# A graph network's neighbour sums on TensorE: from two column halves of up to 64 nodes to four column quarters of up to 32

## The chip, the cores and the metric

The kernel runs on one core of a Trainium2 chip. The metric is the device time of one execution in microseconds. Before the change three runs took 2215.41, 2216.05 and 2217.56 us, median 2216.05 us.

## The reference

There are 6250 nodes with 512 features each and 106,250 directed edges (50,000 random ones in both directions and a loop at every node). Two layers follow each other. Each takes, for every node, the mean of its neighbours' rows, multiplies the mean and the node's own row with a 512 x 512 matrix each, and normalises.

```python
edge_index = jnp.stack([src, dst])
# layer 0
x_l = x @ W_l.T + b_l
agg = segment_sum(x_l[src], dst, num_segments=N_NODES)
deg = segment_sum(ones, dst)
x = _layernorm(x + agg / maximum(deg, 1)[:, None] + x @ W_r.T)
# layer 1: src and dst change roles
msg = h[dst] @ W_neigh.T + b_neigh
neigh = segment_sum(msg, src) / maximum(deg, 1)[:, None]
out = relu(h @ W_self.T + b_self + neigh)
x = _layernorm(h + layernorm(h + out) * ln_gamma + ln_beta)
```

All is in float32. A sum over edges of a product is the product of the sum, so the kernel sums the raw rows first and multiplies the means afterwards. Only the order of the sums differs from the reference.

## The kernel before

The edges are sorted by their target node, and cut into 831 tiles of 128 edges. `place` (L357) finds the first node of every run of seven tiles (`SPAN`), checks that a run meets at most 64 nodes (`H`), and writes a flag; if the flag is not zero, the slow path `plain` is taken, which the data here never does. There are 119 runs. A group `g` is run `g` together with run `60 + g`, so there are 60 groups a layer.

`grouped` (L460) works group by group. For a group:

- `fetch` (L482) gathers the neighbours' rows: one indirect DMA on GpSimd's queue (POOL) for each tile, 128 rows of 2 KB. Seven gathers fill one `rows` buffer; there are six (`CHUNKS`), that is three groups' worth. A gather into a buffer waits until TensorE has read what was there.
- `match` (L495), on VectorE, makes the 0/1 matrices `hot` that say which edge belongs to which of the run's 64 nodes. It reads `s.rel`, which `place` wrote, and the row numbers in PSUM tile `misc`.
- `own_rows` (L534) loads the nodes' own rows through SP's queue, two issues of 64 rows whose start is read from a register.
- `visits` (L547), on TensorE, multiplies `hot` with the rows: 8 tiles for each run (its seven, and the last one of the run before, since a node's edges may begin there). Run `g` uses the left half of TensorE's columns and run `60 + g` the right half, writing to partitions 0 to 63 and 64 to 127 of `agg`. Each float32 matmul is two passes in the trace.
- `shrink` (L502), on ScalarE, makes a bf16 copy of `hot`, and `count` (L560) multiplies it with ones: eight small matmuls give the degrees, in two columns of `misc`.
- `inverse` on VectorE and `average` (L570) on ScalarE make the mean, `turn` (L577) transposes own rows and means on TensorE (eight transposes, `tp`), and `dense` (L582) multiplies both with the weights: 16 passes into `po`.
- `store` (L586) runs `finish0` or `finish1` on VectorE (bias, residual, layer norms) and writes the rows out through SP, two issues of 64 rows. A window may write rows that belong to the next run and that a later group writes again. The last group of each column half writes by an indirect DMA on POOL instead.

The order is written out by hand; each engine executes its own instructions in that order. In turn `g` of the loop (L618) stand: fetch and match of group `g + 1`, own rows, visits, count and average of `g`, at most one step of the other layer's sort that uses TensorE, dense of `g - 1`, turn of `g`, store of `g - 1`, shrink of `g + 1`, up to five sorting steps on VectorE. The sort of layer 1's edges (`Sorter.runs`) is spread over layer 0's groups in this way. VectorE therefore runs, per turn: match of `g + 1`, inverse of `g`, finish of `g - 1`, sorting steps.

Layer 1 gathers from `h_d`, which layer 0 writes, so its first gather waits for layer 0's last store. All of POOL's gathers are issued in program order, and each uses one of eight semaphores in turn, so it also waits for the eighth gather before it to land.

## Time and profile before

| what | value |
|---|---|
| median of three runs | 2216.05 us |
| the profiled execution | 2719.07 us |
| its span, first to last instruction | 2717.3 us |
| TensorE matmul busy | 2071.7 us (76%) |
| TensorE weight loads busy | 861.5 us (32%) |
| VectorE busy | 1047.1 us (39%) |
| ScalarE busy | 390.2 us (14%) |
| GpSimd (POOL) busy | 1594.0 us (59%), 1679 instructions |
| first gather starts at | 28.2 us |
| last gather of layer 0, first of layer 1 start at | 1318.0, 1369.7 us |
| last gather of layer 1 starts at | 2641.0 us |
| mean granted clock of TensorE | 0.899 |

The profiled execution is 503 us longer than the median. Durations below come from it.

How to read the lines: in a group's line stand the source line, the engine, the operation, what it writes and reads, partitions and elements, and the number of instructions; behind the first bar the busy time in us and the mean ns of one; behind the second the idle time of the engine before them, and who ended most of it. PE is TensorE's matmul, PEld its weight load, DVE is VectorE, ACT ScalarE. `128*64` is a matmul on 128 rows and 64 columns of the array. In the order of time stand the start in us, the busy time, the engine, the line, and in brackets the idle time before it and its releaser. `issue` means that the engine waited for nothing that the trace shows. In a chain of waits stand who waited for whom, the us in total, how many times, and the longest.

### The profile page before, as it was taken

The page shows a single profiled execution, that of the slowest core. Times are in us where ns is not written, and L with a number is a line of the kernel's source. Part 1 is how long each engine was busy: PE and PEld are TensorE (multiplying, and loading weights), DVE is VectorE, ACT ScalarE, POOL GpSimd, SP SyncE. Part 2 cuts the span into 40 slices and gives each one's busy share as a digit, 9 for nine tenths or more (in the row PEclk, how much of TensorE's full clock was granted, in tenths as well). Part 3 has the DMA queues.
Part 4 walks back from the last instruction along what each step waited for, and adds up shares of the span by engine and source line. Part 5 has one row for each costly group of instructions (what it writes and reads, how often), then busy time and mean ns, then how long its engine had stood idle before and what let it go on. Part 6 is the DMA issues. An engine that isn't in the chain of part 4 may idle for free.

```text
span 2717.3 us, 23134 instructions
## 1 busy us (share of the span) xinstructions
PE 2071.7 (76%) x7807; PEld 861.5 (32%) x7807; DVE 1047.1 (39%) x2139; ACT 390.2 (14%) x685; POOL 1594.0 (59%) x1679
## 2 busy tenths in 40 slices
PE   2488887778787878888927777778777887877785
PEld 1133333333333333333303333333333333333332
DVE  1344434443434443222302444444444444444444
ACT  0111111111111111111101111111111111111111
POOL 4566665556666565666265566665666666656650
PEclk8789988888898989999968998999899899988998
DMA  7576766666666666676366666666666666666650
GB/s 225 164 204 192 204 199 187 184 182 190 190 191 192 184 196 185 196 214 207 106 178 175 189 192 199 202 201 197 187 202 199 203 200 187 195 189 196 202 174 19
DMA packets 177784, 508.07 MB, mean 187 GB/s; under 512 B 35564, under 2 KB 38054, under 8 KB 177646
## 3 DMA queue, kind: packets, MB, share of 16 engines
q0 software_dynamic: 133456, 437.13, 55.5%
q1 hardware_dynamic: 41358, 63.76, 7.3%
q10 hardware_dynamic: 2832, 5.51, 0.6%
q8 instruction: 66, 1.08, 0.2%
q14 instruction: 72, 0.59, 0.1%
HBM read 475.03 MB, written 31.46 MB: 186 GB/s over the span
## 4 chain that ended last, share of the span: by engine, by line
issue 23%; DVE 9%; PE 8%; SPq 7%; DMA 1%; ACT 1%; another core or an unknown queue 1%; POOLq 0%
PE po L456 6%; SPq L543 4%; SPq L598 2%; DVE po L170 2%; DVE stats L402 2%; SPq L509 2%; DVE po L408 1%; PE tp L447 1%; DVE po L424 1%; DVE po L427 1%; DMA own<-h_d 1%; DVE y L170 1%; PE agg L555 1%; ACT rstd L406 0%
## 5 line engine op out<-in xcount | busy, mean ns | idle before, releaser
L478 POOL DMA_INDIRECT rows<-in_x_dram,idx x831 | 797.0, 959 | 492.3 <-PE agg L555 240.3
L478 POOL DMA_INDIRECT rows<-h_d,idx x831 | 788.7, 949 | 482.5 <-PE agg L555 246.8
L555 PE MATMUL agg<-rows,hot 128*64 128x512 f32 x3792 | 918.2, 613 | 37.9 <-issue 21.7
L456 PE MATMUL po<-wb,ownT 128*128 128x512 f32 x960 | 574.2, 754 | 7.3 <-DVE y L170 6.3
L555 PEld LDWEIGHTS agg<-rows,hot 128*64 128x64 f32 x3792 | 293.8, 140 | 580.4 <-issue 536.8
L456 PE MATMUL po<-wa,meanT 128*128 128x512 f32 x960 | 431.5, 592 | 0.0
L565 PE MATMUL misc<-ones_b,hotb 128*128 128x1 bf16 x960 | 41.5, 164 | 349.1 <-issue 225.7
L456 PEld LDWEIGHTS po<-wb,ownT 128*128 128x128 f32 x960 | 222.2, 243 | 261.3 <-issue 260.1
L424 DVE SCALAR_TENSOR_TENSOR po<-bn,some,po 128x512 f32<-128x512 f32 (+1 forms) x60 | 45.3, 756 | 605.0 <-PE tp L447 264.0
L456 PEld LDWEIGHTS po<-wa,meanT 128*128 128x128 f32 x960 | 181.6, 189 | 234.0 <-issue 234.0
L449 ACT COPY ownT<-tp 128x512 f32<-128x512 f32 x120 | 69.9, 582 | 971.4 <-PE tp L447 497.6
L414 DVE SCALAR_TENSOR_TENSOR po<-bl_t,some,po 128x512 f32<-128x512 f32 (+1 forms) x60 | 45.2, 753 | 406.4 <-PE agg L555 212.9
L574 ACT ACTIVATE mean<-agg,inv 128x512 f32<-128x512 f32 x120 | 82.4, 687 | 788.9 <-DVE some L441 319.6
L438 DVE TENSOR_SCALAR inv<-misc 128x1 f32<-128x1 f32 x120 | 18.9, 158 | 425.7 <-remote 312.2
L170 DVE SCALAR_TENSOR_TENSOR srt<-srt 128x448 f32<-128x448 f32 (+2 forms) x310 | 180.2, 623 | 3.9
L565 PEld LDWEIGHTS <-hotb 128*128 128x128 bf16 x960 | 40.8, 99 | 443.9 <-issue 268.7
L447 PE MATMUL tp<-ident,mean 128*128 128x128 f32 x480 | 77.9, 288 | 123.0 <-ACT mean L574 112.1
L170 DVE SCALAR_TENSOR_TENSOR hot<-rel,misc 128x1024 f32<-128x1024 f32 x120 | 145.2, 1211 | 0.2 <-DVE misc L468 0.2
L447 PE MATMUL tp<-ident,own 128*128 128x128 f32 x480 | 76.0, 276 | 67.5 <-issue 39.3
L504 ACT CAST hotb<-hot 128x1024 bf16<-128x1024 f32 x120 | 123.5, 1029 | 22.6 <-DMA bn<-in_L_gnn_b_neigh_dram 16.1
L406 ACT ACTIVATE rstd<-mv,eps 128x1 f32<-128x1 f32 x180 | 53.0, 295 | 464.0 <-DVE mv L404 343.6
L447 PEld LDWEIGHTS tp<-ident,mean 128*128 128x128 f32 x480 | 58.9, 148 | 131.8 <-ACT mean L574 119.8
(111 smaller groups left out, 841.3 us busy)
## 6 DMA issues: line engine op xcount, KB each, us to landing
own<-h_d SPq DMA_DIRECT2D x119, 128.0 KB
own<-in_x_dram SPq DMA_DIRECT2D x117, 128.0 KB
h_d<-y SPq DMA_DIRECT2D x116, 128.0 KB
out_dram<-y SPq DMA_DIRECT2D x116, 128.0 KB
rows<-in_x_dram,idx POOLq DMA_INDIRECT x831
rows<-h_d,idx POOLq DMA_INDIRECT x831
wa<-in_L_gnn_W_l_dram ACTq DMA_DIRECT2D x1, 1024.0 KB
wb<-in_L_gnn_W_r_dram ACTq DMA_DIRECT2D x1, 1024.0 KB
```

The source lines that it names most:

```text
L170: nc.vector.scalar_tensor_tensor(o, a, 1.0, b, op0=ALU.mult, op1=op)
L402: nc.vector.bn_stats(stats[:nr], v)
L424: nc.vector.scalar_tensor_tensor(po, biases["bn"][:nr], some[:nr], po, op0=ALU.mult, op1=ALU.add)
L447: nc.tensor.transpose(p[:, k, :nr], v[:nr, k * P:(k + 1) * P], ident[:nr, :nr])
L449: nc.scalar.copy(t[:, :, :nr], p[:, :, :nr])
L456: nc.tensor.matmul(po[:nr], a[:, k, :nr], w[:, k, :], start=(i == 0 and k == 0), stop=(i == 1 and k == NK - 1))
L478: nc.gpsimd.indirect_dma_start(out=t, out_offset=None, in_=table, in_offset=bass.IndirectOffsetOnAxis(ap=s.idx[:, m:m + 1], axis=0))
L504: nc.scalar.copy(hb, hots[g])
L543: nc.sync.dma_start(own[H * c:H * (c + 1)], table[ds(start(c * Q + g, table), H), :])
L555: nc.tensor.matmul(agg[H * c:H * (c + 1), :], hot[:, 2 * v + c, :], chunks[g if v else g - 1, c][w * SPAN + v - 1], start=(v == first), st ...
L565: nc.tensor.matmul(st["deg"][:nr], hb[:, 2 * v:2 * v + nr // H, :].rearrange("p c h -> p (c h)"), ones_b, start=(v == 0), stop=(v == VIS - 1))
L574: nc.scalar.mul(mean[:nr], st["agg"][:nr], st["inv"][:nr])
```

## The change

Runs are now half as long: 3.5 tiles (of a pair of runs over seven tiles, one has four tiles of its own and one three, and the tile in the middle is visited by both), with at most 32 nodes. There are 238 runs, and four of them, 60 apart, make a group: 60 groups a layer as before. Run `c * 60 + g` uses column quarter `c`. A group visits five or four tiles for each of its four runs.

Gathered rows are kept by tile: one buffer holds the same tile of all four runs (four gathers), and there are ten. `begin` loads the own rows a turn earlier, in four issues of 32 rows and into three buffers, and `store` writes in four issues. The degrees have their own PSUM tile, `deg`, and the row numbers theirs, `cols`. The dense products are split into an own half and a mean half and stand, for group `g - 1`, between the visits of group `g`; own rows are transposed one turn earlier than means. `po` has one buffer in layer 0 and two in layer 1. The sorting's PSUM tiles are given back before layer 1. `place` computes 238 starts instead of 119, with a selector for the middle row (`mid`) beside the last one, and eight writes of `rel` instead of two.

```diff
-H = 64
-SPAN = 7
-VIS = SPAN + 1
-CHUNKS = 6
+C = 4
+H = P // C
+PAIR = 7
+VIS = PAIR // 2 + 2
+CHUNKS = 10
...
-    NW = (M + SPAN - 1) // SPAN
-    Q = (NW + 1) // 2
+    NW = (2 * M + PAIR - 1) // PAIR
+    Q = (NW + 2 * C - 1) // (2 * C) * 2
...
-            for a, off in ((0, SPAN), (D, SPAN - 1)):
-
-                nc.tensor.matmul(ends[:, a:a + NW - 1], last, bass.AP(
+            ne, no = (NW + 1) // 2, NW // 2
+
+            half = PAIR // 2 + 1
+            for a, sel, off, n in ((0, last, 0, ne), (D // 2, mid, half, no),
+                                   (D, last, PAIR - 1, ne - 1), (D + D // 2, last, half - 1, no)):
+                nc.tensor.matmul(ends[:, a:a + n], sel, bass.AP(
                     tensor=pad.tensor, offset=pad.offset + off,
-                    ap=[list(pad.ap[0]), [SPAN, NW - 1]]), start=True, stop=True)
+                    ap=[list(pad.ap[0]), [PAIR, n]]), start=True, stop=True)
             nc.vector.memset(lo, float(N))
+            nc.vector.tensor_copy(view(lo, (0, 2, ne, 1)), ends[:, :ne].unsqueeze(2))
+            nc.vector.tensor_copy(view(lo, (1, 2, no, 1)),
+                                  ends[:, D // 2:D // 2 + no].unsqueeze(2))
...
-            for i, (w, e) in enumerate(((Q - 2, Q), (NW - 2, NW))):
-                c = bad[:, 2 * NW - 1 + i:2 * NW + i]
-                nc.vector.tensor_tensor(c, lo[:1, e:e + 1], lo[:1, w:w + 1], op=ALU.subtract)
-                nc.vector.tensor_scalar(c, c, float(H), None, op0=ALU.is_lt)
+            for i, e in enumerate([Q * c for c in range(1, C)] + [NW]):
+                t = bad[:, 2 * NW - 1 + i:2 * NW + i]
+                nc.vector.tensor_tensor(t, lo[:1, e:e + 1], lo[:1, e - 2:e - 1], op=ALU.subtract)
+                nc.vector.tensor_scalar(t, t, float(H), None, op0=ALU.is_lt)
...
+            for c in range(C):
+                for i, off in ((0, 0), (1, half)):
+                    nodes = bass.AP(tensor=pad.tensor, offset=pad.offset + PAIR * Q // 2 * c + off,
+                                    ap=[list(pad.ap[0]), [PAIR, Q // 2], [1, VIS]])
+                    rel = self.rel.rearrange("p (q i) v c -> p q i v c", i=2)[:, :, i, :, c]
+                    first = view(lo, (c * Q + i, 2, Q // 2, 1))
+                    nc.vector.tensor_tensor(rel, nodes, first.to_broadcast([P, Q // 2, VIS]),
+                                            op=ALU.subtract)
...
-        p = ps.tile([P, NK, P], F32, name="tp", bufs=2)
+        p = ps.tile([P, NK, P], F32, name="tp")
...
-    def project(ownT, meanT, nr, w_n, w_s, ps):
-        po = ps.tile([P, D], F32, name="po", bufs=1)
-        for i, (a, w) in enumerate(((ownT, w_s), (meanT, w_n))):
-            for k in range(NK):
-                nc.tensor.matmul(po[:nr], a[:, k, :nr], w[:, k, :],
-                                 start=(i == 0 and k == 0), stop=(i == 1 and k == NK - 1))
-        return po
-
-    def grouped(s, table, w_n, w_s, layer, finish, dest, other, sps):
+    def project(po, aT, w, nr, first, end):
+
+        for k in range(NK):
+            nc.tensor.matmul(po[:nr], aT[:, k, :nr], w[:, k, :],
+                             start=first and k == 0, stop=end and k == NK - 1)
...
-            misc = ps.tile([P, H + 2], F32, name="misc", bufs=1)
-            nc.vector.tensor_copy(misc[:, :H], iota[:, :H])
-
-            def halves(g):
-                return [c for c in range(2) if c * Q + g < NW]
-
-            def tiles(g, c):
-                w = c * Q + g
-                return range(w * SPAN, min(M, (w + 1) * SPAN))
+            cols = ps.tile([P, H], F32, name="cols")
+            nc.vector.tensor_copy(cols, iota[:, :H])
+
+            def windows(g):
+                return [c for c in range(C) if c * Q + g < NW]
+
+            def own_tiles(g):
+
+                half = PAIR // 2 + 1
+                return range(g // 2 * PAIR + (half if g % 2 else 0),
+                             g // 2 * PAIR + (PAIR if g % 2 else half))
...
-                if g == 0:
-
-                    first = work.tile([P, D], F32, name="mean")
-                    gather(first, Q * SPAN - 1)
-                    chunks[-1, 1] = {Q * SPAN - 1: first}
-                for c in halves(g):
-                    t = work.tile([P, SPAN, D], F32, name="rows", bufs=CHUNKS)
-                    chunks[g, c] = {}
-                    for i, m in enumerate(tiles(g, c)):
-                        gather(t[:, i, :], m)
-                        chunks[g, c][m] = t[:, i, :]
+                for t in ([-1] if g == 0 else []) + list(own_tiles(g)):
+                    rows = work.tile([P, C, D], F32, name="rows", bufs=CHUNKS)
+                    chunks[t] = {}
+                    for c in windows(g):
+                        m = c * (Q // 2 * PAIR) + t
+                        if 0 <= m < M:
+                            gather(rows[:, c, :], m)
+                            chunks[t][c] = rows[:, c, :]
+
+            def visit_tiles(g):
+                t = own_tiles(g)
+                return range(t.start - 1, t.stop)
 
             def match(g):
-                hot = work.tile([P, VIS * 2, H], F32, name="hot")
-                both(hot, s.rel[:, g].rearrange("p v c -> p (v c)").unsqueeze(2)
-                     .to_broadcast([P, VIS * 2, H]),
-                     misc[:, :H].unsqueeze(1).to_broadcast([P, VIS * 2, H]), ALU.is_equal)
+                hot = work.tile([P, VIS * C, H], F32, name="hot")
+                n = len(visit_tiles(g)) * C
+                both(hot[:, :n], s.rel[:, g].rearrange("p v c -> p (v c)")[:, :n].unsqueeze(2)
+                     .to_broadcast([P, n, H]),
+                     cols.unsqueeze(1).to_broadcast([P, n, H]), ALU.is_equal)
                 hots[g] = hot
...
-            def own_rows(g):
-                own = work.tile([P, D], F32, name="own")
-                n = H * len(halves(g))
-                if g == NW - 1 - Q and table.shape[0] < NP:
+            def begin(g):
+
+                n = H * len(windows(g))
+                own = work.tile([P, D], F32, name="own", bufs=3)
+                state[g] = {"nr": n, "own": own}
+                if g == (NW - 1) % Q and table.shape[0] < NP:
                     nc.gpsimd.indirect_dma_start(
                         out=own[:n], out_offset=None, in_=table,
                         in_offset=bass.IndirectOffsetOnAxis(ap=slots(g, False)[:n, :1], axis=0))
-                    return own
-                for c in halves(g):
+                    return
+                for c in windows(g):
                     nc.sync.dma_start(own[H * c:H * (c + 1)],
                                       table[ds(start(c * Q + g, table), H), :])
-                return own
-
-            def visits(g):
-                agg = state[g]["agg"] = ps.tile([P, D], F32, name="agg")
-                hot = hots[g][0]
-                for v in range(VIS):
-                    for c in halves(g):
-                        w = c * Q + g
-                        first, end = (1 if w == 0 else 0), 1 + len(tiles(g, c))
-                        if first <= v < end:
-                            nc.tensor.matmul(
-                                agg[H * c:H * (c + 1), :], hot[:, 2 * v + c, :],
-                                chunks[g if v else g - 1, c][w * SPAN + v - 1],
-                                start=(v == first), stop=(v == end - 1))
+
+            def visits(g, some):
+
+                if "agg" not in state[g]:
+                    state[g]["agg"] = ps.tile([P, D], F32, name="agg", bufs=2)
+                agg, hot = state[g]["agg"], hots[g][0]
+                for v, t in list(enumerate(visit_tiles(g)))[some]:
+                    for c in windows(g):
+                        ts = [u for u in visit_tiles(g) if c in chunks[u]]
+                        if t in ts:
+                            nc.tensor.matmul(agg[H * c:H * (c + 1), :], hot[:, C * v + c, :],
+                                             chunks[t][c], start=t == ts[0], stop=t == ts[-1])
...
-                st["deg"] = misc[:, H + g % 2:H + g % 2 + 1]
-                for v in range(VIS):
-                    nc.tensor.matmul(st["deg"][:nr],
-                                     hb[:, 2 * v:2 * v + nr // H, :].rearrange("p c h -> p (c h)"),
-                                     ones_b, start=(v == 0), stop=(v == VIS - 1))
-                st["inv"], st["some"] = inverse(st["deg"][:nr], nr, work)
+                deg = ps.tile([P, 1], F32, name="deg")
+                n = len(visit_tiles(g))
...
-            def turn(g):
+                st["mean"] = work.tile([P, D], F32, name="mean")
+                nc.scalar.mul(st["mean"][:nr], st["agg"][:nr], st["inv"][:nr])
+
+            def turn(g, v):
                 st = state[g]
-                for v in ("own", "mean"):
-                    st[v + "T"] = transposed(st[v], st["nr"], v + "T", work, ps)
-
-            def dense(g):
+                st[v + "T"] = transposed(st[v], st["nr"], v + "T", work, ps)
+
+            def dense(g, v):
                 st = state[g]
-                st["po"] = project(st["ownT"], st["meanT"], st["nr"], w_n, w_s, ps)
+                if v == "own":
+                    st["po"] = ps.tile([P, D], F32, name="po", bufs=1 + layer)
+                project(st["po"], st[v + "T"], w_s if v == "own" else w_n, st["nr"],
+                        v == "own", v == "mean")
...
+            begin(0)
             for g in range(Q + 1):
 
 
                 if g + 1 < Q:
                     fetch(g + 1)
                     match(g + 1)
+                    begin(g + 1)
                 if g < Q:
-                    state[g] = {"nr": H * len(halves(g)), "own": own_rows(g)}
-                    visits(g)
+                    visits(g, slice(0, 2))
+                if g:
+                    turn(g - 1, "mean")
+                    dense(g - 1, "own")
+                if g < Q:
+                    visits(g, slice(2, 3))
+                if g:
+                    dense(g - 1, "mean")
+                if g < Q:
+                    turn(g, "own")
+                    visits(g, slice(3, None))
                     count(g)
                     average(g)
-                    more(1, True)
-                if g:
-                    dense(g - 1)
-                if g < Q:
-                    turn(g)
                 if g:
                     store(g - 1)
+                more(1, True)
```

`store` follows the new names and loops over four quarters; the last groups that write by an indirect DMA are those of the four column parts. `plain` calls `project` twice.

## The prediction

> **What bounds the kernel now.** I read the page's busy times first, then the costliest groups, the chain of waits of POOL, and the order of time of POOL and TensorE inside a few groups.
>
> ```profile
> PE 2071.7 (76%) x7807; PEld 861.5 (32%) x7807; DVE 1047.1 (39%) x2139; ACT 390.2 (14%) x685; POOL 1594.0 (59%) x1679
> L478 POOL DMA_INDIRECT rows<-in_x_dram,idx x831 | 797.0, 959 | 492.3 <-PE agg L555 240.3
> L478 POOL DMA_INDIRECT rows<-h_d,idx x831 | 788.7, 949 | 482.5 <-PE agg L555 246.8
> L555 PE MATMUL agg<-rows,hot 128*64 128x512 f32 x3792 | 918.2, 613 | 37.9 <-issue 21.7
> L456 PE MATMUL po<-wb,ownT 128*128 128x512 f32 x960 | 574.2, 754 | 7.3 <-DVE y L170 6.3
> L456 PE MATMUL po<-wa,meanT 128*128 128x512 f32 x960 | 431.5, 592 | 0.0
> ```
>
> By this page TensorE is the bound: 76% busy against 59% of POOL. But POOL's "busy" leaves out the 0.30 us between two gathers. Here is POOL in order of time, and its two largest waits over the run:
>
> ```profile
> 1143.99 0.95 POOL L478 DMA_INDIRECT rows<-in_x_dram,idx  x1 [0.30 <-issue]
> 1145.25 0.95 POOL L478 DMA_INDIRECT rows<-in_x_dram,idx  x1 [0.30 <-issue]
> 1149.43 0.94 POOL L478 DMA_INDIRECT rows<-in_x_dram,idx  x1 [3.24 <-PE agg L555]
> ```
> ```profile
> POOL rows L478 <- PE agg L555: 487.0, 109, 11.8
> POOL rows L478 <- issue: 461.9, 1517, 0.3
> ```
>
> A gather that waits for nothing starts 1.25 us after the last one, all through the run (0.95 + 0.30). So the 1664 gathers (832 a layer) cost at least 1664 x 1.25 = 2080 us, and POOL stood still for another 487.0 us because TensorE had not released a `rows` buffer.
>
> Now the profiled execution is 2719.07 us and the median is 2216.05, 503 us less. Where TensorE held POOL up, it ran like this (weight loads, in order of time):
>
> ```profile
> 1146.14 0.13 PEld L555 LDWEIGHTS agg<-rows,hot 128*64 128x64 f32 x1 [1.09 <-issue]
> 1147.54 0.17 PEld L555 LDWEIGHTS agg<-rows,hot 128*64 128x64 f32 x2 [1.27 <-issue]
> 1148.94 0.21 PEld L555 LDWEIGHTS agg<-rows,hot 128*64 128x64 f32 x4 [1.23 <-issue]
> ```
>
> Steps of 1.40 us, for work that otherwise goes in steps of 0.43 us, waiting for nothing the trace shows; near 445 us SP's register moves step at 0.70 us in the same way. I take these stalls for the recording's own, because 2717.3 - 487.0 = 2230 us, within 15 us of the median: without the stalls POOL would hardly wait, and would set the end by itself. So, unprofiled, **the gather queue paces the kernel**: 13.87 gathers a group x 1.25 = 17.35 us a group.
>
> What is beside it is close. TensorE per group, by the spacing of its starts: sums 8 visits x 2 passes x 0.43 (two column halves run at once: 3792 matmuls of 613 ns took 918.2 us) = 6.9; dense products 16 x 0.43 = 6.9; 8 transposes of 0.11 = 0.9; counts and changes of tile shape 0.5: 15.2 us. The loop through VectorE in layer 1 (VectorE, then TensorE in order of time):
>
> ```profile
> 1752.64 0.76 DVE L424 SCALAR_TENSOR_TENSOR po<-bn,some,po 128x512 f32<-128x512 f32 x1 [9.87 <-PE tp L447]
> ...
> 1761.36 1.22 DVE L170 SCALAR_TENSOR_TENSOR hot<-rel,misc 128x1024 f32<-128x1024 f32 x1
> ```
> ```profile
> 1762.63 0.34 PE L565 MATMUL misc<-ones_b,hotb 128*128 128x1 bf16 x8 [3.11 <-DVE hot L170]
> 1762.83 1.52 PE L456 MATMUL po<-wb,ownT 128*128 128x512 f32 x2
> ```
>
> `finish1` and the next `match` take 9.9 us; the count waits for that `match` (both use tile `misc`), then 0.2 us of count and 6.9 us of dense products lead to the next `finish1`: 17.1 us a group. In layer 0 with five sorting steps it is 10.7 + 7.1 = 17.8 us, otherwise 12 to 14.
>
> **The change, part by part.**
>
> Sums in four column quarters: 5 or 4 visits (4.5 on average) x 4 quarters. If all four run at once, 4.5 x 2 x 0.43 = 3.9 us instead of 6.9: TensorE falls from 15.2 to about 12.4 us a group, with 6 changes of tile shape instead of 3 (0.1 us each between L447's last transpose and L555's first matmul). The number of groups stays 60 a layer (238 runs over 4). The trace has no quarters. From below: halves lose nothing (one pair each 0.43 us). From above: no overlap beyond two, 4.5 x 4 = 18 matmuls x 2 x 0.43 / 2 = 7.7 us. The Trainium skill ("TensorE: Matmul & The Clock Gate", Measured speedup vs the span model) has three column tiles giving only 2.38 times, a loss of a fifth; at that rate 5 us, by the halves' row 3.9. I take the row; with either, and even with 7.7 (16.3 a group), TensorE stays under 17.35 us, so the 3 us saved are worth **nothing directly**: the gathers cover them. If that cover went, they would be worth 3.0 x 120 = 360 us.
>
> Gathers: same 128 rows each, from the same queue; 834 a layer instead of 832 (three borrowed tiles instead of one). +4 x 1.25 = **+5 us**. They now go tile by tile over the four quarters, and a buffer comes free after each four: ten buffers, so POOL waits only if TensorE is some 36 gathers (45 us) behind. `begin` puts one indirect load on POOL as before.
>
> Order of the dense products: the own half and the mean half stand between the visits, so a late gather no longer delays them, and `count` has its own tile, so it no longer waits for `match`. VectorE's loop through the count is gone: `finish` (8.7), `match` (0.8) and the inverse (0.5) must only fit into 17.35 us, with 6 us of sorting in layer 0 too. New waits: `dense(own)` in layer 0 has one `po` and waits for the last group's `finish0` to read it, 0.4 + 1.5 us after the count, while the first two visits (1.7 us) run and wait for gathers anyway; the queue behind it is visits, and POOL feels them only 45 us later. Nothing, then.
>
> SP: 4 loads and 4 stores a group instead of 2 and 2. Two issues take 1.5 us in the trace, so 6 of 17.35 us; loads are issued a group ahead. Nothing; they would cost only from 17 us on.
>
> Head: `place` runs before the first gather. Two more matmuls (0.40 each), a copy (0.28), a compare (0.26), four small operations (0.15 each): **+2 us** (layer 1's copy lies among the gathers). More constants at the start: 0 to 1, under the key loads, 0 taken.
>
> The end of each layer, after the last gather has been issued. Before: landing 2.4, visit 0.9, count and inverse 0.7, old dense 6.9, transposes and copy 1.5, last dense 6.9, `finish0` 3.6, slots 1.5, scatter and first gather 4.4 = 28 us in layer 0; in layer 1 two `finish1` in a row behind the old dense: 40 us with 8 us from the last scatter to the end. After: the old dense is done, so 7 us less; slots of three or four quarters instead of one or two halves, +1.5. 23 and 35 us: **-10 us** together.
>
> Sum. Before: head 28.2 + 833 x 1.25 + 28 + 832 x 1.25 + 40 + 1.8 (launch, 2719.07 - 2717.3) = 2180. The median is 2216, so w = 36 us of other waits are in it. (The profile's own sum: its two ends take 50 and 75 us with their stalls, so 2717 - 487 - 57 = 2173.) After: 30.4 + 835 x 1.2505 + 23 + 834 x 1.2505 + 35 + 1.8 = 2177 us, and what remains of w.
>
> What w is, the trace bounds only: gathers that started 1.26 to 2 us after the last one hold 15 us beyond 1.25, POOL's own, and would stay; the other 21 us I give to the near tie with TensorE and VectorE (17.1 to 17.8 against 17.35), which goes. Ends: all of w goes, 2177; all stays, 2213. I take 2177 + 18 = **2195 us** (-0.9%).
>
> **Rivals.** What a measurement of this kernel can tell from no change is about 0.2% (2212 to 2220).
>
> A: w is the gather queue's own (contention with the other DMAs). For it: the DMA engines are about 0.66 busy, and gathers of 1.3 to 1.6 us are in the trace. Against: only 15 us of them. Then 2213 us, no change.
>
> B: the gather is shorter off the profile, and TensorE and VectorE's loop set the 2216 us. For it: the profile stretches TensorE, so perhaps POOL's 0.30 us gap too. Against: TensorE's matmuls keep 0.43 us wherever they don't stall, and the loops alone make too little: head 28, first gathers 2 x 20, layer 0 60 x 16.4 (half at 17.8, half at TensorE's 15.2) = 984, layer 1 59 x 17.1 = 1010, ends 28 + 40: 2130 us, 86 short of the median, where the gathers' sum is 36 short. At 1.10 us a gather: 30 + 1669 x 1.10 + 23 + 35 + 2 = 1926 us.
>
> C, slower: TensorE waits for gathers in pieces and its clock falls. The skill's clock page (HAM oscillation) wants no idle gap over about 3.4 us and gives half the clock after one; late in a group of the new order TensorE has 0.9 us of work for each 5 us of four gathers, so gaps of 4 us will occur. By the rule, all at half: 24.8 us a group, 60 x 2 x 24.8 + 92 = 3070 us. By the row:
>
> ```profile
> 1100.00:1200.00 100.00, 83.89 (x316) 33.02 (x317) 22.71 (x50) 14.95 (x25) 64.53 (x69) 1.00 0.70 204
> 1400.00:1500.00 100.00, 56.46 (x214) 23.22 (x216) 23.97 (x50) 11.22 (x20) 59.35 (x63) 0.75 0.60 175
> ```
>
> The granted clock (third figure from the end) was 1.00 with TensorE 84% busy and 0.75 with 56%. At 0.75 the group takes 12.4 / 0.75 = 16.5 us, still under the gathers. It decides below 12.4 / 17.35 = 0.71; at 0.66 the group is 18.8 us and the kernel 120 x 18.8 + 92 = 2350 us. A busier TensorE gets its clock back, so I hold it unlikely.
>
> **How the numbers follow.** Forecast (2177 to 2211): 0.68. A: 0.14. B: 0.10. C, or quarters that don't overlap: 0.08. Faster = forecast + B = 0.78; same = A, 0.14; slower 0.08. The likeliest case gives 2195, its own range 2177 to 2211. The range for 8 in 10 runs over A and a small part of B and C: 2135 to 2224.
>
> **What would show it.** Right: POOL's waits for `rows` on L575's sums fall from 487 us to under 150, gathers keep 1.25 us, TensorE's busy time falls and it waits for the gathers' landing; `agg` takes four starts in each 0.43 us. Wrong: a median under 2130 means shorter gathers; over 2224 with a granted clock under 0.75, or `agg` in pairs, means C. The profiled time should fall more than the median, since fewer TensorE instructions stall in it.

## The result, and the profile after

The changed kernel takes 2207.99 us (median of six runs, 2205.10 to 2214.13) beside 2216.11 us for the kernel before: a ratio of 0.9964, 95% interval 0.9949 to 0.9978. In two later series, each on one chip, it was 0.9969 (0.9957 to 0.9980) and 0.9967 (0.9955 to 0.9978). So the change gains 0.3 to 0.4%; all three intervals lie below 1. The prediction said 2195 us, a gain of 0.95%: the sign was right, the size was not.

One thing has to be known to read the runs: on some chips the signals between engines arrive late, and there the kernel before takes 2660 to 2730 us; the profile that the prediction used (2719 us) shows the same delays, and those chips have a section of their own below.

Each ratio is between runs of one series.

The changed kernel's page and its chain of waits (who waits for whom, us in total, how many times, the longest):

```profile
PE 2008.4 (91%) x7871; PEld 668.1 (30%) x7871; DVE 993.7 (45%) x2193; ACT 349.4 (16%) x685; POOL 1600.5 (72%) x1683
L575 PE MATMUL agg<-rows,hot 128*32 128x512 f32 x4272 | 999.9, 608 | 134.7 <-DMA rows<-h_d,idx 53.4
L493 POOL DMA_INDIRECT rows<-in_x_dram,idx x834 | 803.2, 963 | 283.8 <-issue 244.8
L493 POOL DMA_INDIRECT rows<-h_d,idx x834 | 791.1, 949 | 257.0 <-issue 216.3
```

```profile
POOL rows L493 <- issue: 461.1, 1416, 30.0
PEld agg L575 <- DMA rows<-h_d,idx: 268.4, 279, 3.1
PEld agg L575 <- DMA rows<-in_x_dram,idx: 253.0, 305, 2.8
PEld po L470 <- ACT meanT L464: 71.7, 57, 4.4
POOL rows L493 <- PE agg L575: 20.1, 66, 0.3
```

Between the gathers of a layer POOL now waits for nothing beyond its own 0.30 us (the one wait of 30.0 us lies at the start of the run), and TensorE waits 521 us for rows to land: the gather queue paces the kernel. But so it did before. Here are waits from another profile of the unchanged kernel (the run before_fourth below, 2215.03 us), in place of the 487.0 us that the prediction read:

```profile
POOL rows L478 <- issue: 448.5, 1473, 0.3
PEld agg L555 <- DMA rows<-h_d,idx: 255.1, 320, 6.9
POOL rows L478 <- PE agg L555: 21.9, 72, 0.3
```

POOL waits 21.9 us for TensorE's sums in the whole run, 0.3 us at most, no more than its gap between two gathers anyway: in this profile no gap between two gathers of a layer is over 0.32 us. There was nothing to gain at that place.

With both profiles at their true level, the time can be cut in the pieces of the prediction's sum. Head is the start of the first gather. "Slow gathers" is what the steps of the gathers hold beyond the usual step (1.250 us). An end is the rest, up to the next layer's first gather or to the end of the span. The span of before is 2213.3 us, that of the changed kernel 2202.9 us (run after_third, on the same chip):

| us | before, predicted | before, measured | after, predicted | after, measured |
|---|---|---|---|---|
| head | 28.2 | 28.0 | 30.4 | 31.0 |
| gathers at 1.25 | 2081 | 2081 | 2087 | 2086 |
| slow gathers | 15 (in w) | 14 | 15 (in w) | 17 |
| end of layer 0 | 28 | 34.9 | 23 | 23.7 |
| end of layer 1 | 40 | 55.4 | 35 | 44.9 |

The end of layer 0 in before is 1089.75 (first gather of one layer to that of the next) - 833 x 1.25 - 13.6 = 34.9, and so on. The change costs 3 us of head, 5 us of gathers and 3 us of slow ones, and gains 11.2 + 10.5 us in the two ends: 10 us together.

### The profile page after: what moved, and what is told of

Read it like the earlier page. It is cut to its first block, busy times and chain, and to the rows that moved or that the text cites. A ratio compares the mean times of both kernels' runs of the same rounds, so it can differ in the third digit from the quotient of the medians.

```text
span 2212.4 us, 25870 instructions
## 1 busy us (share of the span) xinstructions
PE 2008.4 (91%) x7871; PEld 668.1 (30%) x7871; DVE 993.7 (45%) x2193; ACT 349.4 (16%) x685; POOL 1600.5 (72%) x1683
## 4 chain that ended last, share of the span: by engine, by line
DMA 29%; POOL 27%; PE 24%; issue 14%; DVE 3%; ACT 0%; SPq 0%; POOLq 0%; DVEq 0%
POOL rows L493 27%; DMA rows<-h_d,idx 15%; DMA rows<-in_x_dram,idx 13%; PE po L470 12%; PE agg L575 10%; PE tp L462 2%; DVE po L173 1%; DVE stats L417 0%; PE deg L584 0%; PE turn L270 0%; DVE po L423 0%; DMA own<-h_d 0%; DMA val_i<-in_dst_dram 0%; DVE po L442 0%; DVE y L173 0%
## 5 line engine op out<-in xcount | busy, mean ns | idle before, releaser
L575 PE MATMUL agg<-rows,hot 128*32 128x512 f32 x4272 | 999.9, 608 | 134.7 <-DMA rows<-h_d,idx 53.4
L470 PE MATMUL po<-wa,meanT 128*128 128x512 f32 (+1 forms) x960 | 451.9, 614 | 22.3 <-ACT meanT L464 21.7
L470 PE MATMUL po<-wb,ownT 128*128 128x512 f32 (+1 forms) x960 | 434.4, 595 | 0.1
L575 PEld LDWEIGHTS agg<-rows,hot 128*32 128x32 f32 x4272 | 171.4, 108 | 751.9 <-DMA rows<-h_d,idx 268.4
L470 PEld LDWEIGHTS po<-wa,meanT 128*128 128x128 f32 (+1 forms) x960 | 174.2, 191 | 302.1 <-issue 229.2
L470 PEld LDWEIGHTS po<-wb,ownT 128*128 128x128 f32 (+1 forms) x960 | 173.3, 191 | 174.7 <-issue 174.4
L593 ACT ACTIVATE mean<-agg,inv 128x512 f32<-128x512 f32 (+1 forms) x120 | 82.5, 688 | 421.1 <-DVE some L456 370.6
L173 DVE SCALAR_TENSOR_TENSOR hot<-rel,cols 128x640 f32<-128x640 f32 x120 | 88.8, 742 | 0.5 <-DVE cols L481 0.4
L522 ACT CAST hotb<-hot 128x640 bf16<-128x640 f32 x120 | 78.8, 657 | 27.2 <-DVE hot L173 27.2
L462 PEld LDWEIGHTS tp<-ident,mean 128*128 128x128 f32 (+1 forms) x480 | 51.0, 142 | 104.0 <-issue 46.1
L462 PE MATMUL tp<-ident,mean 128*128 128x128 f32 (+1 forms) x480 | 79.6, 289 | 2.4 <-ACT mean L593 2.4
```

The lines of the kernel that those rows point to most:

```text
L173: nc.vector.scalar_tensor_tensor(o, a, 1.0, b, op0=ALU.mult, op1=op)
L462: nc.tensor.transpose(p[:, k, :nr], v[:nr, k * P:(k + 1) * P], ident[:nr, :nr])
L470: nc.tensor.matmul(po[:nr], aT[:, k, :nr], w[:, k, :], start=first and k == 0, stop=end and k == NK - 1)
L522: nc.scalar.copy(hb[:, :n], hots[g][:, :n])
L575: nc.tensor.matmul(agg[H * c:H * (c + 1), :], hot[:, C * v + c, :], chunks[t][c], start=t == ts[0], stop=t == ts[-1])
L593: nc.scalar.mul(st["mean"][:nr], st["agg"][:nr], st["inv"][:nr])
```

## Undoing the order, keeping the quarters

```diff
                 if g < Q:
-                    visits(g, slice(0, 2))
+                    visits(g, slice(None))
+                    count(g)
+                    average(g)
+                    more(1, True)
                 if g:
-                    turn(g - 1, "mean")
                     dense(g - 1, "own")
-                if g < Q:
-                    visits(g, slice(2, 3))
-                if g:
                     dense(g - 1, "mean")
                 if g < Q:
                     turn(g, "own")
-                    visits(g, slice(3, None))
-                    count(g)
-                    average(g)
+                    turn(g, "mean")
                 if g:
                     store(g - 1)
-                more(1, True)
```

> The changed kernel with quarters, but the dense products of the group before traced after the count again, and own rows and means transposed together, as in the kernel before. At the level of 2216 us for the kernel before: if the 8 us of gain come from the new order at the two ends (step of the sum: the old dense is done when the last gather lands, 7 us at each end), this gives 2215 to 2222 us; if they come from a near tie of TensorE with the gathers, which the quarters end, it stays at 2208 us. At the level of 2707 us: no expectation.

Measured 2226.05 us, where before took 2219.54 and the changed kernel 2213.04 us on the same chip: a ratio of 1.0025 to before (1.0016 to 1.0035), 4 us above what was expected if the gain comes from the order at the ends. The stretch from the last gather of layer 0 to the first of layer 1 is 32.1 us and the tail 54.6 us, against 26.5 and 49.4 in the changed kernel's profile beside it.

So everything in the change but the order of the dense products, the column quarters with it, makes the kernel 6.5 us slower: head, gathers and slow gathers cost 12 us, and the two ends, 37.4 and 56.7 us in the profile before_fourth of another chip, give back 7. The new order gains 13 us, 11 of them in the two ends. This is the step of the prediction that the dense products of the last group but one are done when the last gather lands. There is no near tie in it: the quarters and the degrees' own tile stay in this run, so a near tie would have ended here too.

The changed kernel itself, in the same series:

> The changed kernel unchanged, beside the kernel before on the same chip and in the same minutes as the next three. In the first four experiments the kernel before took 2707 us, not 2216, so it has two levels. If TensorE's and SP's stalls (steps of 0.70 us, semaphores late by 8 us) belong to the executions there and not to one recording, a level of 2707 us for the kernel before comes with a changed kernel of 2550 to 2650 us (fewer instructions on TensorE per group, but the same stalls); a level of 2216 us comes with 2208 us.

Measured 2213.04 us beside 2219.54.

## What the gathers hide

Half of the gathers are left out in both kernels. The sums of the other half use rows that are there already, so both outputs are other ones; TensorE and VectorE do all their work.

```diff
-                            gather(rows[:, c, :], m)
-                            chunks[t][c] = rows[:, c, :]
+                            from_ = c - 2 if c - 2 in chunks[t] else c
+                            if from_ == c:
+                                gather(rows[:, c, :], m)
+                            chunks[t][c] = rows[:, from_, :]
```

> The changed kernel with half of its gathers left out: quarters 2 and 3 of a group sum the rows gathered for quarters 0 and 1 (so the output is another one); TensorE, VectorE and the own rows keep all their work. Theory 1 (the gather queue at 1.25 us per gather paces both kernels and hides what TensorE saves): the queue needs only 8.7 us a group, so TensorE's 12.4 us a group come to light: 120 x 12.4 + 92 for head and ends = 1580 us, up to 1700 where VectorE with the sort is longer. Theory 2 (TensorE and VectorE's loop set a good part of the time): a small fall, over 2050 us. Theory 3 (the bytes of the DMA pace, not the issues): as theory 1.

> The kernel before with half of its gathers left out in the same way (the right half sums the rows gathered for the left half). The loop by the trace is 17.1 us a group in layer 1 and 16.4 on average in layer 0: about 2130 us, no more than 90 us under the kernel before. Theories 1 and 3: the difference to the changed kernel with half its gathers is then 400 to 550 us, which is TensorE's and VectorE's gain that the gathers hide. Theory 2: both kernels differ as little here as with all gathers, by some 10 us.

Measured 1941.59 us for the changed kernel and 2201.37 us for the kernel before (the chip has late signals with all gathers; both profiles show them on time but for two of 120 groups). The hidden gain exists, 260 us, but it is half of what was expected. Between the first and the last gather a layer takes 793.6 and 979.0 us in the changed kernel, 1008.8 and 1031.1 us in the one before: 13.2 and 16.3 us a group against 16.8 and 17.2. In layer 0 the gain is near what the working said. In layer 1 it isn't, because of a loop that the working took for gone. TensorE, then ScalarE, of the changed kernel with half the gathers, in order of time (start, busy time, in brackets the idle time before and its releaser):

```profile
1299.66 1.07 PE L577 MATMUL agg<-rows,hot 128*32 128x512 f32 x8
1303.38 5.40 PE L470 MATMUL po<-wa,meanT 128*128 128x512 f32 x8 [2.65 <-ACT meanT L464]
...
1317.09 1.07 PE L577 MATMUL agg<-rows,hot 128*32 128x512 f32 x8
1320.70 5.40 PE L470 MATMUL po<-wa,meanT 128*128 128x512 f32 x8 [2.55 <-ACT meanT L464]
```

```profile
1314.85 0.29 ACT L421 ACTIVATE rstd<-mv,eps 128x1 f32<-128x1 f32 x1 [2.39 <-DVE mv L419]
1319.37 0.29 ACT L421 ACTIVATE rstd<-mv,eps 128x1 f32<-128x1 f32 x1 [4.23 <-DVE mv L419]
1319.57 0.60 ACT L524 CAST hotb<-hot 128x512 bf16<-128x512 f32 x1
1320.08 0.58 ACT L464 COPY meanT<-tp 128x512 f32<-128x512 f32 x1
```

The transposes of the mean are done by 1313.7, but ScalarE copies them out only at 1320.08: in its queue stand, ahead of that copy, the two square roots of `finish1` of the group before, and `finish1` takes VectorE 8.7 us. TensorE waits 2.6 us, and then runs the product of the means in part at half speed (5.40 us instead of 3.60; so in 53 of the 60 groups). The loop closes because VectorE takes up the next `finish1` behind the inverse of the next group, and the count for that stands behind this product on TensorE. Its period is 17.4 and 16.4 us in turn (groups of five and of four tiles), 16.8 us in the mean. The kernel before, with half its gathers, has its own loop, through `match` and the count: the visits start at 1511.37 and again at 1528.74, 17.37 us later, and so in most groups (19.1 us in 12 of 59, around an own product at half speed). So the change cut one loop of 17.4 us and made another of 16.8 us. With all gathers in place both stay hidden, but barely: a full group of before has 14 gathers, 17.5 us, and in before_fourth `finish1` starts every 17.5 us.

## Less work for TensorE, and a slower kernel

The prediction gave 21 us of the 36 that its sum left over to a near tie with TensorE and VectorE's loop. To test it, every second visit of the sums was left out of the kernel before, with all gathers kept (the sums miss those edges):

```diff
-                        if first <= v < end:
+                        end -= (end - 1 - first) % 2
+                        if first <= v < end and (v - first) % 2 == 0:
```

> The kernel before with every second visit of the sums left out (the sums miss those edges); gathers, dense products and VectorE stay. TensorE needs 11.7 us a group instead of 15.2. The prediction gave 21 of the 36 us that the sum does not explain to a near tie with TensorE and VectorE's loop, which goes when TensorE needs less. By that step: 2190 to 2200 us at the level of 2216. If those 36 us are the gather queue's own slow gathers and longer ends: 2208 to 2216 us. At the level of 2707 us: if TensorE's instructions stall there, fewer of them stall, so clearly less than 2707.

Measured 2381.02 us, 7% slower than before (1.0708 to 1.0744): less work, more time, which neither theory had. The trace shows why. TensorE, then VectorE:

```profile
1508.31 3.65 PE L556 MATMUL agg<-rows,hot 128*64 128x512 f32 x16
1517.57 0.35 PE L566 MATMUL misc<-ones_b,hotb 128*128 128x1 bf16 x8 [5.60 <-DVE hot L170]
1517.78 6.56 PE L456 MATMUL po<-wb,ownT 128*128 128x512 f32 x8
```

```profile
1507.55 0.76 DVE L424 SCALAR_TENSOR_TENSOR po<-bn,some,po 128x512 f32<-128x512 f32 x1 [9.23 <-PE po L456]
...
1516.31 1.21 DVE L170 SCALAR_TENSOR_TENSOR hot<-rel,misc 128x1024 f32<-128x1024 f32 x1
...
1527.81 0.75 DVE L424 SCALAR_TENSOR_TENSOR po<-bn,some,po 128x512 f32<-128x512 f32 x1 [9.44 <-PE po L456]
```

In this stretch `finish1` starts 20.26 us after the one before (1507.55, 1527.81), 19.9 us in the mean of the layer. `finish1` and `match` take 9.9 us, then come the count and the dense products. TensorE, with fewer sums, now stands idle for 5.60 us before the count, and after that idle time the granted clock is a half (third figure from the end; busy times by engine before it):

```profile
1503.00:1517.00 14.00, 8.97 (x35) 3.85 (x34) 8.35 (x15) 2.60 (x5) 8.64 (x10) 0.99 0.65 184
1517.00:1523.00 6.00, 5.43 (x14) 2.37 (x14) 0.90 (x4) 0.69 (x1) 4.60 (x5) 0.50 0.89 278
```

The first eight passes take 6.56 us instead of 3.68. The loop of 17.4 us has become one of up to 20.4 us, longer than the gathers, and paces layer 1. With all visits (before_fourth, 1200 to 2150 us) the granted clock is 1.00. This is rival C's mechanism, in the kernel before instead of the changed one, and with VectorE as what TensorE waits for.

The loop was meant to be cut, with the visits still out, by a PSUM tile of its own for the degrees (the transposes give up one of their two buffers for it):

```diff
-                st["deg"] = misc[:, H + g % 2:H + g % 2 + 1]
+                st["deg"] = ps.tile([P, 1], F32, name="deg", bufs=1)
```

> The kernel before with every second visit of the sums left out (the sums miss those edges), as in the run that took 2381 us, and the degrees in a PSUM tile of their own, so that the count no longer waits for VectorE's match (the transposes have one buffer instead of two for it). If 2381 us come from the loop finish, match, count, dense products through VectorE, lengthened because TensorE idles 6 us before the dense products and runs them at half clock (20.3 us a group instead of 17.1), cutting the loop brings the gathers' pace back: 2195 to 2225 us. If it comes from the missing visits in another way, it stays over 2330 us.

It fell on a chip with late signals: 2890.54 us beside 2676.45 us. That does not tell the two theories apart. The loop is read from the trace; that cutting it brings the time back was not shown.

## The kernel before at its own level

> The kernel before unchanged, as in the run before_third: at the level of 2216 to 2220 us head 28.2, gathers of layer 0 1055 us, gap 31 to 36, layer 1 1040, tail 50 to 58 if the 36 us are slow gathers and long ends; over 2112 us for the gathers of both layers, and over 20 us of POOL's waits for TensorE's sums, if a near tie with TensorE and VectorE's loop holds a part.

Measured 2215.40 us (2213.48 to 2216.63). Its parts are in the table above. A near tie costs nothing here: the gathers of layer 1 take 1038.85 us for 831 steps of 1.25 (1038.75). What the sum missed is in the ends. TensorE in the last 60 us, where the last gather is issued at 2156.59:

```profile
2155.41 3.68 PE L456 MATMUL po<-wb,ownT 128*128 128x512 f32 x8
2158.93 3.60 PE L456 MATMUL po<-wa,meanT 128*128 128x512 f32 x8
...
2163.33 7.08 PE L555 MATMUL agg<-rows,hot 128*64 128x512 f32 x16
2171.57 0.41 PE L565 MATMUL misc<-ones_b,hotb 128*64 128x1 bf16 x8 [1.16 <-ACT hotb L504]
2171.91 3.70 PE L456 MATMUL po<-wb,ownT 128*128 128x512 f32 x8
...
2185.98 5.92 PE L456 MATMUL po<-wb,ownT 128*64 128x512 f32 x8 [6.29 <-DVE y L170]
```

The working let one visit (0.9 us) follow the last landing. But the last group has only one run, seven gathers in 8.75 us, and when they are all issued TensorE is still at the dense products of group 57, two before the last; all visits of the last group follow (7.08 us, 6.2 more than the working had). And the last own product waits 6.29 us for VectorE's `finish1` to give the one `po` buffer back, and then runs in part at half speed (5.92 us; the granted clock is 0.50 there). In layer 0 the visits take 7.08 us too, but the wait is 1.03 us and the product keeps its speed. That fits ends that are 15.4 and 6.9 us longer than predicted, though the 40 us of the working aren't itemised enough to set them off term by term. The changed kernel is rid of part of this: in layer 1 its own product of the last group needs no buffer back, and the old dense products are done.

## The changed kernel's tail

The changed kernel's tail (51.2 us in the first profile, 49.4 and 46.1 us in two others) is longer than the 36 us of the working, by the loop through ScalarE's queue that the half gathers showed. TensorE's last two products of means, in two profiles of the changed kernel on its own, the one with a tail of 46.1 us first, then that with 49.4:

```profile
2163.52 5.37 PE L470 MATMUL po<-wa,meanT 128*96 128x512 f32 x8 [2.55 <-ACT meanT L464]
2179.21 3.67 PE L470 MATMUL po<-wa,meanT 128*96 128x512 f32 x8 [3.53 <-ACT meanT L464]
```

```profile
2164.35 5.15 PE L470 MATMUL po<-wa,meanT 128*96 128x512 f32 x8 [2.56 <-ACT meanT L464]
2179.83 5.37 PE L470 MATMUL po<-wa,meanT 128*96 128x512 f32 x8 [3.53 <-ACT meanT L464]
```

The same wait of 3.53 us is followed by a product at full speed in one and partly at half speed in the other. A first attempt against the waits wrote the last group of each layer in another order (only the lines that change it):

```diff
+                if last:
+                    store(g - 1)
                 turn(g, "own")
                 visits(g, slice(3, None))
+                if last:
+                    dense(g, "own")
                 count(g)
                 average(g)
+                if last:
+                    turn(g, "mean")
+                    dense(g, "mean")
+                    store(g)
```

> The changed kernel with the last group of each layer written in another order: store of group 58 before the last sums, own dense product of group 59 before its count, mean transposed and multiplied at once, so that ScalarE's copy of the transposed mean does not stand behind the two square roots of the finish of group 58. If the tail of layer 1 (51 us after the last gather, where 36 were predicted) is long because of that queue, this takes 8 to 15 us off: 2193 to 2200 us at the level of 2216. If it is long for another reason (TensorE behind the gathers), under 4 us.

Measured 2219.16 us beside 2213.04 for the changed kernel: not 8 to 15 us less, but 6 more. ScalarE in the tail of this run (the two square roots, the copy, and the mean, which waits for the count):

```profile
2183.53 0.29 ACT L421 ACTIVATE rstd<-mv,eps 96x1 f32<-96x1 f32 x1 [8.65 <-DVE mv L419]
2188.02 0.29 ACT L421 ACTIVATE rstd<-mv,eps 96x1 f32<-96x1 f32 x1 [4.19 <-DVE mv L419]
2188.22 0.46 ACT L464 COPY ownT<-tp 128x384 f32<-128x384 f32 x1
2194.76 0.68 ACT L593 ACTIVATE mean<-agg,inv 96x512 f32<-96x512 f32 x1 [6.09 <-DVE some L456]
```

The store was traced ahead of `turn(g, "own")`, so now the copy of the own rows stood behind the square roots, and the count, which follows the own product on TensorE, with it. The edit moved the fault to another copy. The second attempt traces the store of every group behind the transpose of the next mean (`own` gets a fourth buffer, `mean` one instead of two):

```diff
                 if 0 < g <= Q:
                     turn(g - 1, "mean")
+                if g > 1:
+                    store(g - 2)
                 if 0 < g <= Q:
                     dense(g - 1, "own")
...
-                if g:
-                    store(g - 1)
```

> The changed kernel with the store of every group traced half a turn later, behind the transpose of the next mean, so that on ScalarE the copy of the transposed mean never stands behind the two square roots of a finish (the order of the run with the reordered last group put another copy, of the own rows, behind them). Theory that ScalarE's queue makes the two ends long: the gap between the layers 24 to 27 us and the tail 36 to 42 us (from 26.5 and 49.4), so 8 to 14 us less than the changed kernel, 2199 to 2206 us on a chip where that takes 2213. Theory that TensorE is behind at the ends for another reason: no change.

> The changed kernel with the store traced half a turn later, as before this. Where the kernel before takes 2216 to 2220 us: by the theory of ScalarE's queue gap 24 to 27 us, tail 36 to 42 us, 2197 to 2206 us in all; by the other, as the changed kernel, 2207 to 2213 us. Where the kernel before takes 2670 to 2710 us: 2676 us again.

On two chips with late signals: 2676.18 us beside 2676.45 (ratio 0.9986 to 1.0025), and 2699.38 beside 2709.77 (0.9945 to 0.9979). The trace of the first shows a cost in layer 0: there `po` has one buffer, the own product waited 201 us in all for the delayed `finish0`, and layer 0's gathers took 1322 us where the kernel with 1 KB rows below had 1226 on that chip (the changed kernel itself was not run there). So the late store, and its buffers, were kept for layer 1 alone:

```diff
-            for g in range(Q + 1):
+            for g in range(Q + 2 if layer else Q + 1):
...
+                if layer and g > 1:
+                    store(g - 2)
...
-                if g:
+                if g and not layer:
                     store(g - 1)
```

> The changed kernel with the store traced half a turn later in layer 1 alone, so that ScalarE's copy of the transposed mean stands ahead of the two square roots of the finish. At the level of 2216 to 2220 us for the kernel before: by the theory that this queue makes the tail long, a tail of 36 to 42 us instead of 49 to 51 and 2197 to 2206 us in all; by the other theory as the changed kernel. On a chip with late semaphores: the changed kernel's time beside it less 10 to 20 us.

> The changed kernel unchanged. At the level of 2216 to 2220 us for the kernel before: 2207 to 2213 us. On a chip with late semaphores (the kernel before at 2670 to 2710): as with 1 KB rows, 2600 to 2630 us, so 3% less than the kernel before, because the waits that TensorE's late signals make are fewer where the dense products don't stand behind the count.

Measured 2196.62 us (2192.60 to 2197.73) beside 2206.31 for the changed kernel and 2215.40 for the one before: 0.9909 of before (0.9892 to 0.9925). The tail is 37.0 us, where the changed kernel beside it has 46.1; every other part agrees within 1.2 us. ScalarE around the last gathers, first of the changed kernel, then with the late store:

```profile
2157.77 0.29 ACT L421 ACTIVATE rstd<-mv,eps 128x1 f32<-128x1 f32 x1 [2.39 <-DVE mv L419]
2162.29 0.29 ACT L421 ACTIVATE rstd<-mv,eps 128x1 f32<-128x1 f32 x1 [4.22 <-DVE mv L419]
2162.49 0.60 ACT L522 CAST hotb<-hot 128x512 bf16<-128x512 f32 x1
2163.00 0.47 ACT L464 COPY meanT<-tp 128x384 f32<-128x384 f32 x1
```

```profile
2154.01 0.61 ACT L522 CAST hotb<-hot 128x512 bf16<-128x512 f32 x1
2155.85 0.48 ACT L464 COPY meanT<-tp 128x384 f32<-128x384 f32 x1 [1.23 <-PE tp L462]
2156.48 0.29 ACT L421 ACTIVATE rstd<-mv,eps 128x1 f32<-128x1 f32 x1 [0.15 <-DVE mv L419]
2161.00 0.29 ACT L421 ACTIVATE rstd<-mv,eps 128x1 f32<-128x1 f32 x1 [4.22 <-DVE mv L419]
```

The copy now comes ahead of both square roots, 7 us earlier, and TensorE goes through to its last product without the waits of 2.55 and 3.53 us. This version beats both kernels.

## Bytes or issues

Each gather with half its bytes: once as 128 rows of 1 KB (each sum uses the 256 features twice), once as 64 rows of 2 KB (the sums run over half of the edges). The main lines of the two edits, cut:

```diff
-                    out=t, out_offset=None, in_=table,
+                    out=t, out_offset=None, in_=table.rearrange("n (h d) -> (n h) d", h=2),
...
```

```diff
-                    in_offset=bass.IndirectOffsetOnAxis(ap=s.idx[:, m:m + 1], axis=0))
+                    in_offset=bass.IndirectOffsetOnAxis(ap=s.idx[:P // 2, m:m + 1], axis=0))
...
-                            gather(rows[:, c, :], m)
-                            chunks[t][c] = rows[:, c, :]
+                            gather(rows[:P // 2, c, :], m)
+                            chunks[t][c] = rows[:P // 2, c, :]
...
```

> The changed kernel with all gathers, each still 128 descriptors, but of 1 KB rows instead of 2 KB (every table row is read as two of 256 features, and each sum uses the 256 features twice, so the output is another one and TensorE's work is the same). Theory 1 (POOL's issue of 1.25 us per gather paces): 2190 to 2208 us, no less than 2185, gathers still 1.25 us apart. Theory 3 (bytes pace, since the DMA engines are 0.81 busy): the gathers come closer, 1.0 us or less apart, and the time falls below 2000 us, down to TensorE's 1580.

> The changed kernel with all gathers, but 64 rows of 2 KB in each instead of 128 (the sums run over the first 64 edges of each tile, so the output is another one; TensorE has as many passes). Same bytes as the run with 1 KB rows, half the descriptors. Theory 1 in the form that a gather's cost is per instruction: 1.25 us apart, 2190 to 2208 us. Theory 1 in the form that POOL's 0.95 us are spent per row: 0.3 + 0.48 = 0.8 us apart and TensorE becomes the bound, 1580 to 1700 us. Theory 3: as the run with 1 KB rows, below 2000 us in both.

> The changed kernel with 1 KB rows. Where the kernel before takes 2216 to 2220 us: theory 1 (POOL's issue paces) gathers 1.25 us apart and 2190 to 2213 us; theory 3 (bytes pace) below 2000 us. The 17 us of slow gathers in layer 0 should shrink if they are contention for the DMA engines, and stay if they are POOL's own.

All of them, and a further one with 1 KB rows, fell on chips with late signals: with 1 KB rows 2614.89 us beside 2707.57 for the kernel before, 2607.63 beside 2676.45 and 2618.38 beside 2709.77, with 64 rows 2619.62 beside 2707.57. The totals can't be used, but the steps can. POOL with 1 KB rows, where nothing holds it up:

```profile
599.44 0.95 POOL L493 DMA_INDIRECT rows<-in_x_dram,idx  x1 [0.30 <-issue]
600.69 0.95 POOL L493 DMA_INDIRECT rows<-in_x_dram,idx  x1 [0.30 <-issue]
```

With half the bytes a gather still takes 1.25 us (1426 of 1672 steps lie between 1.24 and 1.26 us; the DMA engines move 111 GB/s in the mean instead of 230). With half the rows the median step is 1.21 us. So the pace is neither the bytes nor, but for 0.04 us, the number of rows: it is nearly all per instruction.

## Chips with late signals

> The kernel before unchanged, for a second profile. The prediction laid the 500 us between the profiled execution and the median to the recording. If it is so, a new profile is 2700 us again beside a median of 2216 to 2220. If it belongs to some executions or chips, the profile is near the median, SP's steps of 0.70 us are gone, and the parts can be read directly: by the prediction's sum head 28.2, 832 gathers at 1.25 us, 28 us, 832 gathers, 40 us, 2180 in all; by the theory that the 36 us left over are slow gathers (about 17) and longer ends (about 20), the gap between the layers is 31 to 36 us and the tail 52 to 58.

Measured 2677.09 us in 20 runs, and 2708.08 us on another chip in a run of the same kind (before_third). So the stalls are not the recording's: on three of the five chips of the experiments every run with all its gathers has them, and on the other two none has. The chip of the prediction's profile, and of the three runs at 2216 us beside it, is not on record. The sign in the trace is ScalarE's copy of the transposed own rows. It starts 0.04 us after the transposes end in the profiles at the level of 2200 us (but for at most three of 120 groups, where ScalarE was still busy), and 1.3 us (median) and up to 38.7 us after them in before_again. ScalarE in the profile that the prediction used:

```profile
1149.07 0.58 ACT L449 COPY ownT<-tp 128x512 f32<-128x512 f32 x1 [13.18 <-PE agg L555]
```

The transposes had ended by 1141.5. With half the gathers, on a chip where the kernel before takes 2707 us, the copies come 0.04 us after them again (within 0.15 us, but for two of 120 groups in each profile), and with half the bytes or half the rows per gather they don't (medians of 2.7 and 3.8 us). So it goes with how many gathers are issued, not with what each moves. What delays the signals there stays open, and so does what the change itself is worth on such a chip, since the changed kernel itself was only measured on others.

## Why the prediction was off

Two terms of the sum failed. The left-over of 21 us was given to a near tie that costs nothing, while it sat in the two ends of the kernel before, which the working had 22 us too short. And after the change the end of layer 1 takes 44.9 us where the working said 35, because ScalarE's queue was put at nothing.

- **What bounds the kernel** was right: the gather queue, 1.25 us per gather, 0.95 busy and 0.30 between. But the evidence was misread on the way. The stalls in the profile were laid to the recording; on three chips all runs of this kernel take 2660 to 2730 us. The 487 us of waits, 109 of them, belong to that level; at 2216 us they are 21.9 us. The bound came out right all the same, since the stalls were taken out of the sum, whatever makes them.
- **The quarters are worth nothing directly**: right. With the old order they cost 6.5 us. The working had +5 for gathers and +2 for the head; measured are +5 and +3, and +3 of slow gathers. All four quarters run at once where their rows lie ready, as the row of the halves had it, without the loss of a fifth that the row of the Trainium skill ("TensorE: Matmul & The Clock Gate", Measured speedup vs the span model) would give: 16 passes on `128*32` in the run with half gathers take 1.92 us, four starts lie within each 0.43 us.
- **Ends -10 us**: mis-sized. They are -22 us, because the ends of before are 34.9 and 55.4 us, not 28 and 40. The term of the sum that failed is "landing 2.4, visit 0.9, ... old dense 6.9" for the kernel before: the short last group leaves TensorE behind, its visits take 7 us, and in layer 1 the last own product waits 6.3 us for `po` and runs partly at half clock.
- **"The other 21 us I give to the near tie with TensorE and VectorE's loop, which goes"**: this step failed. A near tie is there (a loop of 17.37 us in most groups against 14 gathers, 17.5 us, in a full group; the 13.87 of the working count the short last group in), but it costs nothing: no gap between gathers is lengthened by it. Those 21 us are the mis-sized ends, 22 us. Of them 12 go and 10.6 stay, so that w is 28 us after the change (17 slow gathers, 10.6 in the ends, 1 in the head), where the forecast left 18.
- **"VectorE's loop through the count is gone"**: true, but the sentence that `finish`, `match` and the inverse "must only fit into 17.35 us" overlooked ScalarE. The own half and mean half were separated, and the mean's copy got behind `finish1` on ScalarE's queue. That is the 10 us in the last end: with the copy ahead, the end of layer 1 is 35.7 us, where the working said 35, and the whole takes 2196.6 us, where it said 2195. That number is no proof of the near tie: the 18 us of w that the forecast let stay happen to be the slow gathers and the head, and the rest was let go for a wrong reason.
- **Rival A** (the gather queue's own w, no change) had part of the cause: 14 of the 36 us are slow gathers in before, 17 us after. **Rival B** (shorter gathers) is out, they keep 1.25 us on every chip. **Rival C** did not come: the granted clock is 0.98, and TensorE's waits for rows are at most 3.1 us, but for 9.6 us once. Its mechanism is real, though: half clock after some 5.6 us of idle time in 59 of 60 groups of layer 1 in the kernel with fewer visits. The Trainium skill ("TensorE: Matmul & The Clock Gate", HAM oscillation) puts the idle gap at about 3.4 us; here waits of 2.55 to 2.65 us in ScalarE's loop were enough for a slow product, while one of 3.53 us in a tail was enough in one profile (5.37 us for the eight passes after it) and not in another (3.67 us).
- **What would show it**: waits for `rows` under 150 and gathers at 1.25 us came true, but they were true of before as well, at its own level, and so told nothing. TensorE's busy time did not fall (1983.6 us before at its own level, 2008.4 after). Where rows land one by one, 1.25 us apart, the passes run singly instead of four at once: the sums are busy for 999.9 us in the changed kernel and for 570.6 us with half the gathers, for as many passes. Whether the profiled time falls more than the median can't be told from profiles of two levels.

## What to carry to other kernels

Before a left-over of a sum is given to a cause, look for it where the sum is worked out by hand: here in the two ends of the pipeline, where short last groups, a single PSUM buffer and a halved clock make most of 22 us. When one engine's loop is cut, follow the same work through the queue of every engine that it passes; an in-order queue with one slow reader in front (two square roots of a 9 us chain) makes a new loop almost as long as the old. And a profile that is much slower than the timed runs should be taken again, on another chip, before it is read for waits.

## What was not expected of the hardware

- Less work for TensorE made the kernel 7% slower; the trace shows idle time and a halved clock in the loop that then paces it.
- After the same wait TensorE's clock is halved in one execution and not in the next: of three waits of 2.55 to 3.54 us at the end of layer 1 in the changed kernel, one is followed by a slow product of means in one profile (run after_third) and all three in another (run after); the tails are 46.1 and 51.2 us.
- Signals between engines come late on some chips (ScalarE wakes up to 38 us late) while gathers are issued every 1.25 us, and nearly always on time with half as many gathers; the kernel before takes 21 to 22% longer there.
- The cost of an indirect gather of 128 rows is POOL's, 1.25 us, nearly whatever it moves: 1.25 us with 1 KB rows, 1.21 us with 64 rows.
- 55 of the 835 gathers in layer 0 take about 1.0 to 1.4 us instead of 0.95, 9 in layer 1 (run after_third). VectorE sorts in layer 0; whether that is the reason was not tried.
- From one execution to another the usual step of a gather is 1.250 or up to 1.253 us (run after_tail), 5 us over the kernel.
